# Two row buffers in place of three for a group of attention queries, with the rest written over the scaled queries

## The chip, the cores and the metric

The kernel runs on one core of one Trainium2 chip. The metric is the device time of one execution in microseconds. The time before is 1096.12 us, the median of three runs (1095.92 to 1096.5). A profile of one more execution gives the time of every instruction on the five engines: PE (matmuls), DVE, ACT, POOL (each works through its own queue in order) and SP, which only issues DMAs.

## The reference

Two layers with gates work on x (4 batches, 512 tokens, 512 channels) and a context of the same shape. The names below are those of the reference, cut to the steps.

```python
x = x + tanh(g_xattn[0]) * wkv(w, u, k=layernorm(x), v=ctx)          # a scan over the tokens
x = x + tanh(g_ffn[0])   * bitlinear_ffn(layernorm(x), w1, w2, w3)   # 1 bit weights, int8 groups
x = x + tanh(g_xattn[1]) * attention(layernorm(x), ctx, wq, wkv, wp) # 16 heads of 32
x = x + tanh(g_ffn[1])   * ternary(layernorm(x), gamma, W)           # rms norm, ternary weights
# in attention:
q = qdq(x) @ qdq(wq).T + bq            # 512 queries of a batch, 512 channels
attn = softmax(q k^T / sqrt(32))       # per head
out = qdq(attn v) @ qdq(wp).T + bp
```

## The kernel before, in words

The four batches go through four stages each: the scan (`wkv_layer`), the feed-forward layer (`ffn_layer`), the attention (`attention_layer`) and the closing ternary layer (`ternary_layer`). Each stage is a generator, and a planner (`line`, `place`, `run`) takes steps of all of them in the order of places that are written out by hand. So the attention of batch b runs beside the feed-forward layer of batch b+1 and the scan of batch b+2. The Tile framework then puts the recorded instructions into the queues of the engines, by its own estimate of when each could start, with a buffer that is free at that point; `in_turn` and `next_turn` hold matmuls to the recorded order of the steps. A queue runs in order, so an instruction that waits holds back everything behind it on its engine.

Attention of one batch takes the channels in four groups of 128 (four heads each). `project(g)` makes the queries of a group: four bf16 matmuls into `q_ps` (line 162 through the helper `matmul`), then on DVE the scaled queries `at_q` (line 898), on ACT the half `at_half[0]`, which is `at_q` plus the bias rounded to the short float format (line 903), and on DVE the rest, `at_q` plus bias minus that half (line 904). Both halves go to DRAM (`qD`, line 908, two DMAs on SP), from where `fetch_queries` (line 913, through `stack`) brings them back as `at_qR` in the layout of the score matmuls. Groups 0 and 1 are projected ahead of the loop over the 16 units of a batch, group 2 in unit 0 and group 3 in unit 4.

All of these row tiles come from one ring: `row(...)` in `attention_layer` is a tile of 128x512 floats of the pool `att` with the tag `at_row` and `ROWS = 3` buffers. The same ring serves `at_xn` (the normalised input of the attention, lines 219, 222, 231), `at_y` (line 1036, batches 0 and 1) and, in batches 0 and 1, `tf_xn` of the ternary layer. A buffer comes free when its last reader is done: for `at_q` that is line 904, for the halves the DMA that stores them, for `tf_xn` the PE transposes (`qr_ps`, line 165).

The ternary layer of a batch works on four token tiles t. For batches 0 and 1 a tile passes POOL twice (line 219: centred; line 1147: times gamma), DVE for its largest magnitude (line 222) and four small steps on a 128x1 column (lines 1151, 1152, 1159, 1158), ACT for the rounding (line 231), PE for four transposes (`qr_ps`), ACT again (line 238) and PE for `f_ps`; line 1172 adds the result to x and line 1173 stores it. This layer of batch 0 runs while the attention of batch 1 is in its units around group 3, and the layer of batch 1 beside the attention of batch 2.

Other lines that the prediction names: scan: 599 and 634 (DVE scans), 608, 630, 635, 636, 641, 642 (POOL), 640 (DVE reciprocals), 645 (DVE product); feed-forward: 685 (POOL), 745 (ACT), 746 and 750 (DVE), 697 (DVE); attention: 948 (DVE, negated row maximum of the scores), 950 (ACT, exponentials), 970 (ACT, copies the transposed probabilities), 1000 (DVE, output into `at_o`); layer norm: 180 and 207 (POOL), 191, 194, 200 and 204 (DVE).

Of the kernel before, what the change touches and what calls it, by code (L numbers as in the profile page):

```python
# [11 lines left out]
F32R = mybir.dt.float32r  # L12
# [18 lines left out]
def kernel(  # L31
# [99 lines left out]
    def bank(name, dtype=F32):  # L131

        return psum_tile(name, "m", dtype)
# [27 lines left out]
    def matmul(*args, **kwargs):  # L161
        return in_turn(nc.tensor.matmul(*args, **kwargs))  # L162
# [677 lines left out]
    def attention_layer(b, xb, pool, tiles=range(NT)):  # L840
# [5 lines left out]
        lo, n = tiles[0] * P, len(tiles) * P  # L846
# [9 lines left out]
        def row(name, dtype=F32):  # L856
            return pool.tile([P, D], dtype, name=name, tag="at_row", bufs=ROWS)
# [29 lines left out]
        def project(g):  # L887
            qp = bank("q_ps")[:, 0:n]
            for c in range(NC):
                matmul(  # L890
                    qp,
                    lhsT=wqT[:, c, g * P : (g + 1) * P],
                    rhs=xqT[:, c, lo : lo + n],
                    start=(c == 0),
                    stop=(c == NC - 1),
                )
            q = row("at_q")[:, 0:n]
            nc.vector.scalar_tensor_tensor(
                q, qp, sq[:, g : g + 1], sxb[:, lo : lo + n], ALU.mult, ALU.mult
            )  # L900
            half = [row("at_half", F32R)[:, 0:n] for _ in range(2)]
            bias = bqc[:, g : g + 1]
            nc.scalar.activation(half[0], q, AF.Identity, bias=bias)
            nc.vector.scalar_tensor_tensor(
                half[1], q, bias, half[0].bitcast(F32), ALU.add, ALU.subtract
            )
            for i in range(2):
                nc.sync.dma_start(out=qD[b][g][i, :, lo : lo + n], in_=half[i].bitcast(F32))
# [83 lines left out]
        def collect(k):  # L992
# [14 lines left out]
            )  # L1007

        project(0)
        fetch_keys(0)  # L1010
        fetch_values(0)
        fetch_queries(0)
        yield
        project(1)
        fetch_queries(1)
        yield
# [45 lines left out]
        for k in range(len(units) + 2):  # L1062
# [29 lines left out]
            if now:  # L1092
                p, h = units[k]
                if h == 0:
                    if p + 1 < NP:
                        fetch_keys(p + 1)
                    if p % 2 == 0 and p // 2 + 2 < NC:
                        next_turn()
                        project(p // 2 + 2)
                elif p % 2 and p // 2 + 1 < NC:  # L1100
                    fetch_values(p // 2 + 1)
                if k + 2 < len(units):
                    fetch_queries(k + 2)
# [320 lines left out]
```

## Time and profile before

| what | value |
|---|---|
| time, median of 3 runs | 1096.12 us (1095.92 to 1096.5) |
| the profiled execution's own time | 1094.21 us |
| its span, first to last instruction | 1092.4 us |
| PE busy | 943.3 us, 86% of the span |
| DVE busy | 827.0 us, 76% |
| ACT busy | 729.9 us, 67% |
| POOL busy | 320.7 us, 29% |
| mean granted TensorE clock | 0.956 |
| line 904 | 16 instructions, 742/752/1764 ns (min/median/max) |
| line 903 | 16 instructions, 713/724/760 ns |
| line 908, DMA `qD<-at_half` | 32 issues, 2.0/2.2/4.1 us to landing |
| line 219 on `tf_xn` | 8 instructions, 762/768/772 ns |

Busy time of PE is the time in which a matmul is under way; matmuls overlap, so that is not PE at its peak. The granted clock is the share of TensorE's full clock. A line of a timeline gives the start from the beginning of the span, the time of the merged run of instructions, engine, line, operation, output<-inputs, shape and count, and in brackets the idle time of the engine before it with what ended it.

### The profile page before, as it was taken

Reading aid. Unit: us, or ns where it says so; the run is one execution under the profiler, and the core shown is the slowest. Engines: PE = TensorE matmul, PEld = TensorE weight load, DVE = VectorE, ACT = ScalarE, POOL = GpSimd, SP = SyncE. Lnnn points to the kernel's source line nnn. Section 1 sums busy time; section 2 is a strip of 40 time slices with the busy share of each in tenths; the row PEclk is TensorE's granted clock in tenths of the full one; section 3 lists DMA queues with packets and bytes.
Section 4 is the critical chain, followed back from the end, with each engine's and each line's share of the span. In section 5 each row is a group of like instructions: output and inputs, shape, how many; then the busy total and the mean of one; then the engine's idle time right before and its main releaser. Section 6 shows DMA issues by size and latency. Waiting matters only on the chain.

```text
span 1092.4 us, 17928 instructions
## 1 busy us (share of the span) xinstructions
PE 943.3 (86%) x6350; PEld 680.0 (62%) x6380; DVE 827.0 (76%) x1600; ACT 729.9 (67%) x1490; POOL 320.7 (29%) x328
## 2 busy tenths in 40 slices
PE   3879997998879888799997886999999999878975
PEld 2345564565557666677775665677776777655652
DVE  5985548757876899896769898966687866579976
ACT  5656755567545776667877576677685777877863
POOL 3831104423333254621215545412122410100000
PEclk8889999999999999999999798999999999989998
DMA  8188845464445674645576354655574563244311
GB/s 288 39 272 317 323 169 190 144 221 155 154 146 181 221 234 127 231 129 169 185 234 204 121 177 133 204 195 180 184 231 156 184 210 116 59 148 116 116 42 39
DMA packets 85674, 189.68 MB, mean 174 GB/s; under 512 B 12241, under 2 KB 36817, under 8 KB 74577
## 3 DMA queue, kind: packets, MB, share of 16 engines
q1 hardware_dynamic: 85584, 188.53, 51.7%
q8 instruction: 51, 0.84, 0.3%
q14 instruction: 39, 0.31, 0.1%
HBM read 148.65 MB, written 39.85 MB: 173 GB/s over the span
## 4 chain that ended last, share of the span: by engine, by line
PE 49%; DVE 22%; ACT 14%; POOL 5%; issue 5%; DMA 4%; SPq 1%; ACTq 0%; POOLq 0%; DVEq 0%
PE ff_hp L162 15%; PE pt_ps L165 7%; PE ff_acc L162 6%; PE o_ps L162 4%; PE v_ps L162 4%; PE s_ps L162 3%; ACT at_P L950 3%; DVE wk_q L640 3%; ACT at_PT L970 3%; DVE at_nm L948 2%; PE k_ps L162 2%; DVE wk_p L634 1%; PE qr_ps L165 1%; PE tp_ps L165 1%; ACT wk_e L612 1%
## 5 line engine op out<-in xcount | busy, mean ns | idle before, releaser
L162 PE MATMUL ff_hp<-wT,xp 128*128 128x512 f32 x1024 | 275.7, 412 | 6.6 <-DVE ff_z L746 3.7
L162 PEld LDWEIGHTS ff_hp<-wT,xp 128*128 128x128 f32 x1024 | 195.4, 196 | 54.6 <-DVE ff_z L746 5.7
L950 ACT ACTIVATE at_P<-s_ps,at_nm 128x512 f32<-128x512 f32 x256 | 175.0, 690 | 45.2 <-DVE at_nm L948 43.4
L948 DVE TENSOR_REDUCE at_nm<-s_ps 128x1 f32<-128x512 f32 x256 | 166.6, 677 | 38.4 <-PE s_ps L162 37.9
L970 ACT COPY at_PT<-pt_ps 128x512 f32<-128x512 f32 x224 | 131.2, 590 | 72.6 <-PE pt_ps L165 71.9
L685 POOL TENSOR_TENSOR ff_z<-qg_b,qg_s 128x512 f32<-128x512 bf16 x64 | 71.9, 1124 | 314.6 <-ACT qg_b L684 304.7
L165 PE MATMUL pt_ps<-ident,at_P 128*128 128x128 f32 x1024 | 155.4, 280 | 9.0 <-ACT at_PT L970 4.3
L165 PEld LDWEIGHTS pt_ps<-ident,at_P 128*128 128x128 f32 x1024 | 118.1, 142 | 47.3 <-ACT at_PT L970 10.9
L162 PE MATMUL ff_acc<-wT,hr 128*128 128x512 f32 x512 | 137.6, 409 | 5.2 <-DVE hr L697 2.6
L162 PE MATMUL s_ps<-at_kR,at_qR 128*128 128x512 f32 x256 | 103.0, 464 | 24.0 <-ACT at_P L950 17.6
L162 PEld LDWEIGHTS ff_acc<-wT,hr 128*128 128x128 f32 x512 | 92.9, 191 | 26.2 <-DVE hr L697 4.2
L162 PE MATMUL o_ps<-at_PT,at_V 128*32 128x128 f32 x2048 | 75.4, 281 | 4.7 <-ACT at_PT L970 2.8
L162 PEld LDWEIGHTS o_ps<-at_PT,at_V 128*32 128x32 f32 x2048 | 54.8, 111 | 28.6 <-issue 11.6
L746 DVE SCALAR_TENSOR_TENSOR ff_z<-ff_z,ff_hp 128x512 f32<-128x512 f32 x64 | 43.4, 679 | 37.0 <-ACT ff_z L745 36.9
L745 ACT ACTIVATE ff_z<-ff_hp,coef 128x512 f32<-128x512 f32 x64 | 44.1, 688 | 40.5 <-PE ff_hp L162 38.1
L750 DVE SCALAR_TENSOR_TENSOR ff_z<-ff_hp,coef,ff_z 128x512 f32<-128x512 f32 x64 | 47.7, 745 | 30.2 <-PE ff_hp L162 30.1
L684 ACT CAST qg_b<-qg_i 128x512 bf16<-128x512 int8 x80 | 49.3, 617 | 27.4 <-DVE qg_i L680 17.3
L162 PEld LDWEIGHTS s_ps<-at_kR,at_qR 128*128 128x128 f32 x256 | 43.3, 194 | 36.4 <-ACT at_P L950 25.2
L162 PE MATMUL v_ps<-wkvT,cT 128*128 128x512 f32 x128 | 60.5, 618 | 5.5 <-DVE wT L303 2.3
L162 PE MATMUL k_ps<-cT,wkvT 128*128 128x512 f32 x128 | 61.3, 631 | 2.3 <-ACT wk_k L584 1.0
L640 DVE RECIPROCAL wk_q<-wk_q 128x256 f32<-128x256 f32 x32 | 54.5, 1722 | 3.0 <-POOL wk_q L635 1.6
L696 ACT CAST hr<-tp_ps 128x512 fp32r<-128x512 f32 x64 | 37.6, 588 | 21.7 <-PE tp_ps L165 21.7
(180 smaller groups left out, 1669.4 us busy)
## 6 DMA issues: line engine op xcount, KB each, us to landing
wT<-wD SPq DMA_DIRECT2D x72, 1024.0 KB, 5.4
wn<-in_L_ffn_w_dram SPq DMA_DIRECT2D x18, 1024.0 KB, 6.2
at_kR<-kD SPq DMA_DIRECT2D x128, 128.0 KB, 4.0
at_qR<-qD SPq DMA_DIRECT2D x256, 64.0 KB, 2.5
wD<-wT SPq DMA_DIRECT2D x12, 1024.0 KB, 4.2
kD<-k_half SPq DMA_DIRECT2D x16, 512.0 KB, 2.8
qD<-at_half SPq DMA_DIRECT2D x32, 256.0 KB, 2.2
cn<-in_ctx_dram SPq DMA_DIRECT2D x8, 512.0 KB, 5.9
```

Source lines behind the costliest of these rows:

```text
L162: return in_turn(nc.tensor.matmul(*args, **kwargs))
L165: return in_turn(nc.tensor.transpose(*args))
L640: nc.vector.reciprocal(half, half)
L684: nc.scalar.copy(qb, qi)
L685: nc.gpsimd.tensor_tensor(grouped(src), grouped(qb), s.unsqueeze(2).to_broadcast([P, NG, GS]), ALU.mult)
L696: nc.scalar.copy(part[:, 0, :], pt)
L745: nc.scalar.activation(z, hp, AF.Tanh, scale=coef[:, 0:1])
L746: nc.vector.scalar_tensor_tensor(z, z, 1.0, hp, ALU.add, ALU.mult)
L750: nc.vector.scalar_tensor_tensor(z, hp, coef[:, 1:2], z, ALU.mult, ALU.mult)
L948: nc.vector.tensor_reduce(nm, sp, AX.X, ALU.max, negate=True)
L950: nc.scalar.activation(lanes[k, i, t], sp, AF.Exp, bias=nm, accum_out=sums[k][:, t, i : i + 1],)
L970: made[k] = nc.scalar.copy(dst, blocks(pt))
```

## The change

The second of the two halves no longer takes a buffer of its own from the ring. It is the buffer of the scaled queries `q`, seen in the short float format; line 904 reads `q` and writes over it, and the second DMA of line 908 stores it from there. A group takes two buffers of the ring in place of three.

```diff
@@ -898,7 +898,7 @@
             nc.vector.scalar_tensor_tensor(
                 q, qp, sq[:, g : g + 1], sxb[:, lo : lo + n], ALU.mult, ALU.mult
             )
-            half = [row("at_half", F32R)[:, 0:n] for _ in range(2)]
+            half = [row("at_half", F32R)[:, 0:n], q.bitcast(F32R)]
             bias = bqc[:, g : g + 1]
             nc.scalar.activation(half[0], q, AF.Identity, bias=bias)
             nc.vector.scalar_tensor_tensor(
```

## The prediction

> **What bounds the kernel now.** I read the page first, then all waits of PE, then the timelines of PE, DVE, POOL and SP around the groups whose line 904 moves. Shares of engines:
>
> ```profile
> PE 943.3 (86%) x6350; PEld 680.0 (62%) x6380; DVE 827.0 (76%) x1600; ACT 729.9 (67%) x1490; POOL 320.7 (29%) x328
> ```
>
> PE sets the end, and what counts is the places where it waits. The waits of PE (engine, tile, line, releaser: us in total, times, longest us) hold one at which the ring of the change stands:
>
> ```profile
> PE qr_ps L165 <- ACT tf_xn L231: 16.2, 4, 8.6
> ```
>
> The timeline of PE (start, us, operation, in brackets the idle time before it and its releaser) shows this wait of 8.60 us at 661.05, and three spots that the change also reaches:
>
> ```profile
> 661.05 1.11 PE L165 MATMUL qr_ps<-ident,tf_xn 128*128 128x128 f32 x4 [8.60 <-ACT tf_xn L231]
> ...
> 858.91 0.66 PE L165 MATMUL qr_ps<-ident,tf_xn 128*128 128x128 f32 x4
> ...
> 870.53 0.66 PE L165 MATMUL qr_ps<-ident,tf_xn 128*128 128x128 f32 x4 [0.86 <-ACT at_PT L970]
> ...
> 961.64 1.19 PE L162 MATMUL s_ps<-at_kR,at_qR 128*128 128x512 f32 x2 [3.37 <-DMA at_qR<-qD]
> ```
>
> The ring was full at the first: line 904 of group 3 (batch 1) stood at 662.27, behind `qr_ps` of tile 0, because its buffer was that tile's; SP's store of it held SP's queue for 9.6 us from 653.44, and POOL's passes for tiles 1 and 2 came after that, at 663.13.
>
> **What the change moves.** I compared the order in which both built programs issue on each engine. The counts are the same and nothing differs before some 640 us; three places differ: A, tiles of batch 0 beside group 3 of batch 1; B, tiles of batch 1 beside group 3 of batch 2; C, groups 0 and 1 of batch 3.
>
> *Place A.* Line 904 now comes directly behind line 680 of 644.37, and SP's store of the rest goes out one fetch behind the half's (643.67), so the 9.6 us of SP's waiting are gone. PE gains nothing from that: over the whole span it waits for `at_qR` 4.2 us in 3 times, 3.37 of them at 961.64. The buffers are free early, so both POOL passes of tiles 1 and 2 move up, between POOL's line 685 of 646.14 and line 642 of the scan. POOL and DVE before (two timelines):
>
> ```profile
> 646.14 1.49 POOL L685 TENSOR_TENSOR ff_z<-qg_b,qg_s 128x512 f32<-128x512 bf16 x1
> ...
> 652.47 1.26 POOL L642 TENSOR_TENSOR wk_e<-wk_e 128x512 f32<-128x512 f32 x1
> ...
> 658.38 1.62 POOL L608 TENSOR_TENSOR wk_p<-wk_k,wk_o 128x512 f32<-128x512 f32 x1 [2.65 <-DVE wk_o L599]
> ...
> 663.13 1.52 POOL L219 TENSOR_SCALAR tf_xn<-xb,ln_r 128x512 f32<-128x512 f32 x2
> 664.61 2.52 POOL L1147 TENSOR_TENSOR tf_xn<-tf_xn,gamma_b 128x512 f32<-128x512 f32 x2
> ```
> ```profile
> 654.89 0.68 DVE L645 TENSOR_TENSOR wk_e<-wk_e,wk_q 128x512 f32<-128x512 f32 x1
> ...
> 657.09 1.21 DVE L599 TENSOR_TENSOR_SCAN wk_o<-wc,wk_k 128x512 f32<-128x512 f32 x1
> ...
> 658.88 1.15 DVE L1159 TENSOR_TENSOR tf_s<-tf_s,coef 128x1 f32<-128x1 f32 x1
> ...
> 660.03 0.12 DVE L1158 TENSOR_SCALAR tf_s<-tf_s 128x1 f32<-128x1 f32 x1
> ```
>
> POOL ran without a gap from 644.59 to 653.73, so two passes by 0.76 and two by 1.26, 4.04 us, come on top: line 642 ends at 657.77 instead of 653.73. Line 645, which needs it, had 1.16 us in hand (654.89) and moves by 2.88. Behind it on DVE stands the chain that frees line 231 of tile 0 on ACT and so `qr_ps`; it ends with line 1158. On this stretch DVE gets one more line 222 (0.60 from start to start, as at 655.49 to 656.09), and loses line 599, which moves behind line 1158 (1.13, from 657.09 to the next at 658.22), and a line 998 (0.09). Line 1159 took 1.15 us where its fellows take 0.14, and ended with POOL's line 608 (660.00); this pass follows line 599, so it is gone from there: −1.0. Together 2.88 + 0.60 − 1.13 − 0.09 − 1.0 = +1.26. In this stretch PE ran at half clock (the windows: us, busy time of PE, PEld, DVE, ACT, POOL, then the granted clock, the DMA share and GB/s; the last two rows are from the neighbourhood of 834 us):
>
> ```profile
> 656.27:659.68 3.41, 0.00 (x0) 0.00 (x0) 3.41 (x9) 0.62 (x1) 1.30 (x1) 0.50 0.31 75
> ...
> 833.77:837.18 3.41, 1.82 (x12) 1.27 (x11) 3.41 (x10) 2.41 (x6) 0.00 (x0) 1.00 0.00 0
> 837.18:840.59 3.41, 3.41 (x9) 2.31 (x8) 2.72 (x9) 1.36 (x3) 0.00 (x0) 0.50 0.00 0
> ```
>
> The clock stood at 0.50 until 666.51, so 1.26 us of lost PE time are 0.63 us of work at full clock: **+0.63**. Lower bound −1.06: POOL and ACT have tiles 1 to 3 ready earlier, and the two line 231 that stand on ACT near 678 (0.85 and 0.84) leave the queue in front of an `f_ps` that waited 2.2 us there. Upper bound +2.3: one more window at half clock, 3.41/2 = 1.7. I take the middle, since the windows near 675 were busy 1.90 and 2.00 of 3.41 and kept full clock.
>
> The Trainium skill ("SBUF — State Buffer", section "Who interferes with whom") lets the second of a DVE instruction with two inputs in SBUF and a POOL instruction that reads SBUF wait until the first is done. Line 1159's 1.15 us agree, line 219 on `tf_xn`, never over 0.772 us, shows no such wait; by the rule the four passes put among the scan's DVE products would cost still more.
>
> *Place B.* Before, POOL stood idle at the time:
>
> ```profile
> 851.59 1.04 POOL L685 TENSOR_TENSOR ff_z<-qg_b,qg_s 128x512 f32<-128x512 bf16 x1 [7.76 <-ACT qg_b L684]
> ...
> 860.46 1.52 POOL L219 TENSOR_SCALAR tf_xn<-xb,ln_r 128x512 f32<-128x512 f32 x2 [6.76 <-DVE qg_s L676]
> ```
> ```profile
> 855.75 1.29 DVE L948 TENSOR_REDUCE at_nm<-s_ps 128x1 f32<-128x512 f32 x2 [1.57 <-PE s_ps L162]
> ...
> 857.84 0.75 DVE L750 SCALAR_TENSOR_TENSOR ff_z<-ff_hp,coef,ff_z 128x512 f32<-128x512 f32 x1 [0.79 <-PE ff_hp L162]
> 858.50 0.28 DVE L1000 TENSOR_TENSOR at_o<-ot_ps,at_rt 128x128 f32<-128x128 f32 x1
> ```
>
> So POOL's passes cost POOL nothing, but DVE's magnitudes of tiles 1 and 2 (line 222) now stand ahead of the pair of line 948 and wait for POOL: line 685 ends 852.63, then tile 1 (0.77 + 1.29) to 854.69, lines 180 and 207 (0.7 + 0.2) to 855.6, tile 2 (0.77 + 1.29) to 857.7. Line 222 of tile 2 then occupies DVE to 858.4, and the pair of line 948 starts there, 2.65 later than 855.75. Behind it: the pair 1.2, four small steps 0.46, line 750 0.66, line 1000 0.28, each from start to start: line 1000 ends at 861.0 instead of 858.78. `qr_ps` now waits for that line, whose PSUM bank it takes (before, for ACT): PE idles **+2.2**. The window from 857.66 to 861.07 falls from 3.28 us busy to some 1.1. The rows above show a window of 1.82 busy followed by one at 0.50, so I count half a window more, +1.7. Back comes the 0.86 idle at 870.53, as that tile is rounded earlier. Sum 2.2 + 1.7 − 0.86 = **+3.0**; bounds −0.9 (the wait is covered by work that PE takes meanwhile, the payback stays) and +3.9 (no payback); without the clock +1.3.
>
> The Trainium skill ("TensorE: Matmul & The Clock Gate", section "HAM oscillation — how this bites in real kernels") asks for no idle gap above about 3.4 us; by it a gap of 2.2 costs no clock, B is 1.3 and the forecast 1098.7. The row of 833.77, whose longest gap was 0.95 us, speaks against the rule.
>
> *Place C.* DVE now takes line 898 of group 1 ahead of line 904 of group 0 (954.86 and 955.72 before, 0.75 each). Line 898 needs the last `q_ps` matmul (954.80), so line 904 starts near 955.52 instead of 954.86: **+0.66**, which passes the store (2.2 to landing) to the fetch of 958.04 and so to the 3.37 us wait of PE at 961.64. Bounds 0 (ACT's line 903 hides part) and 0.75.
>
> *The write in place* costs nothing by itself: same instruction, same shape, and DVE has others that write over an input in the time of those that don't (line 645, 0.68). No one else reads the scaled queries after line 904; its wait for line 903 stood there already, so no new wait is added.
>
> *Sum.* 0.63 + 3.0 + 0.66 = +4.3 on the profiled execution: 1094.21 + 4.3 = 1098.5 (span 1092.4 + 4.3 = 1096.7). That execution is 1.91 below the median of the runs, and I carry this: **1100.4**. The bounds add to −2.0 (−1.06 − 0.9 + 0) and +6.95 (2.3 + 3.9 + 0.75), so 1094.1 to 1103.1.
>
> **Rivals.** *Slower still* (0.18): A loses a window of clock too, +1.7, in all +6.0: 1102.1. For it: 656.27 is already at 0.50 and more idle follows it; against: the windows near 675 kept full clock.
>
> *Nothing to be measured* (0.22): the ring still has three buffers, so the change only renames who waits, or B's 2.2 us straddle two windows, cost no clock, and A's round-off earlier pays: 1.3 + 0.66 − 1.06 = +0.9, some 1097. For it: DVE at B has 1.57 and 0.79 idle ahead of the lines concerned; against: 4.04 us of POOL work in a stretch with no gap.
>
> *Faster* (0.14), the other side: POOL's moved passes hide. If line 642 still ends before 654.89, DVE's chain at A is shorter by 1.13 + 0.09 + 1.0 − 0.60 = 1.62, PE restarts at 659.4, ahead of the window border 659.68, and gets full clock one window earlier (1.7); the 1.62 count half (0.81), B gives only its payback, −0.86, C takes 0.66: −2.7, 1093.4. It decides from 1.16 us of added POOL time on. For it: POOL idles 2.83 us ahead of 644.59 and 1.9 after 653.73; against: the order puts tile 1 behind line 685 of 646.14, where no gap is.
>
> **How the numbers follow.** Forecast 0.46, slower still 0.18, nothing 0.22, faster 0.14. A measurement tells 0.2%, 2.2 us, from no change. The sum's bounds, 1094.1 to 1103.1, leave out the faster case and small ends. Faster by over 0.2% is that case, 0.14; within 0.2% the second rival and a little of the forecast's lower end, 0.24; slower 0.62.
>
> **What would show it.** Profile after: line 642 near 656.5 and `qr_ps` near 662.3 with over 9 us of idle (A); the pair of line 948 near 858.4, `qr_ps` near 861 behind an idle time of 2 us and a window at 0.50 behind it (B); `s_ps` near 962 plus what A and B added (C); SP's 9.6 us gone. It is wrong if the scheduler's early tiles free PE from waits after 663 that I bounded at 2 us, or if the clock of a window goes otherwise than the rows above let expect.

## The result and the profile after

| | before | after |
|---|---|---|
| median of the runs | 1095.72 us (16 runs, 1093.12 to 1096.5) | 1097.79 us (16 runs, 1095.98 to 1100.57) |
| profiled execution, span | 1094.21 us, 1092.4 us | 1097.88 us, 1096.0 us |

The ratio is 1.0025, 95% interval 1.0016 to 1.0033: slower by about 2.7 us. A second comparison in other runs gave 1.0025 again (1.0016 to 1.0034); one of its runs took 1629.73 us at a mean clock of 0.72, is a slow one, and is left out here and below. The forecast was 1100.4 us, range 1094.1 to 1103.1.

The shares of the engines hardly move; the instructions are the same:

```profile
PE 942.4 (86%) x6350; PEld 679.7 (62%) x6380; DVE 827.7 (76%) x1600; ACT 731.3 (67%) x1490; POOL 320.9 (29%) x328
```

The waits of PE after the change (engine, tile, line, releaser: us in total, times, longest us) show the known wait grown from 8.6 to 9.9 us, and one that was not there before:

```profile
PE qr_ps L165 <- ACT tf_xn L231: 17.9, 4, 9.9
...
PE qr_ps L165 <- DVE at_o L1000: 2.3, 1, 2.3
```

The timeline of PE gives their places, A and B, and the matmuls after the third place, C (start, us, operation, idle time before it and its releaser):

```profile
662.89 1.11 PE L165 MATMUL qr_ps<-ident,tf_xn 128*128 128x128 f32 x4 [9.88 <-ACT tf_xn L231]
...
860.52 0.66 PE L165 MATMUL qr_ps<-ident,tf_xn 128*128 128x128 f32 x4 [2.33 <-DVE at_o L1000]
...
964.72 1.19 PE L162 MATMUL s_ps<-at_kR,at_qR 128*128 128x512 f32 x2 [4.16 <-DMA at_qR<-qD]
```

How late is PE? I matched the runs of matmuls of the two profiles in their order and took the difference of their starts. From 282 to 645 us it stays within 0.25 us. Then: +0.99 between 645 and 700 us (A), −1.59 between 830 and 850, +2.87 between 850 and 875 (B), +0.97 between 951 and 975 (C), and 0.34 from 1069 us on; together the 3.6 us of the spans. The −1.59 is a window of the clock: the profile of before has TensorE's clock at half speed from 837.18 to 840.59, and this one has not; other profiles have it either way (below).

### The profile page after: what moved, and what is told of

Read it like the earlier page. It is cut to its first block, busy times and chain, and to the rows that moved or that the text cites. A ratio compares the mean times of both kernels' runs of the same rounds, so it can differ in the third digit from the quotient of the medians.

```text
span 1096.0 us, 17923 instructions
## 1 busy us (share of the span) xinstructions
PE 942.4 (86%) x6350; PEld 679.7 (62%) x6380; DVE 827.7 (76%) x1600; ACT 731.3 (67%) x1490; POOL 320.9 (29%) x328
## 4 chain that ended last, share of the span: by engine, by line
PE 46%; DVE 24%; ACT 13%; POOL 6%; DMA 5%; issue 5%; SPq 1%; POOLq 0%; ACTq 0%; DVEq 0%
PE ff_hp L162 14%; PE pt_ps L165 7%; PE ff_acc L162 5%; PE o_ps L162 4%; PE s_ps L162 4%; DVE wk_q L640 3%; ACT at_P L950 3%; PE v_ps L162 3%; ACT at_PT L970 2%; DVE at_nm L948 2%; PE k_ps L162 2%; DVE wk_p L634 2%; PE qr_ps L165 1%; PE tp_ps L165 1%; DVE qg_i L680 1%
## 5 line engine op out<-in xcount | busy, mean ns | idle before, releaser
L750 DVE SCALAR_TENSOR_TENSOR ff_z<-ff_hp,coef,ff_z 128x512 f32<-128x512 f32 x64 | 47.7, 746 | 30.1 <-PE ff_hp L162 29.9
L950 ACT ACTIVATION_READ_ACCUMULATOR at_P<-s_ps,at_nm 128x1 f32 x256 | 52.2, 204 | 0.0
```

The source lines that it names most:

```text
L750: nc.vector.scalar_tensor_tensor(z, hp, coef[:, 1:2], z, ALU.mult, ALU.mult)
L950: nc.scalar.activation(lanes[k, i, t], sp, AF.Exp, bias=nm, accum_out=sums[k][:, t, i : i + 1],)
```

## The experiments

Each run's span times its mean granted clock is called the time at full clock below, the rest of the span the clock's part. This is an account and no cause: a half window in which PE waits anyway counts in the clock's part and costs little. "The whole change" is the changed kernel.

**One batch at a time.** The in-place write is given to one batch only; the other batches keep three buffers.

```diff
-            half = [row("at_half", F32R)[:, 0:n], q.bitcast(F32R)]
+            half = [row("at_half", F32R)[:, 0:n], q.bitcast(F32R) if b == 0 else row("at_half", F32R)[:, 0:n]]
```

(and `b == 1`, `b == 2`, `b == 3`). Batch 0 alone changes no engine's order, batch 1 alone changes it at A only, batch 2 at B only, batch 3 at C only.

> The rest is written in place in batch 0 alone (4 of the 16 groups); in this kernel no engine's order of instructions differs from the kernel before. Theory (the write itself is free, only moved work costs): time as before, ratio 1.000 within 0.001, no place of PE later than before by over 0.3 us beyond what the clock's windows do, line 904 at 742 to 752 ns as before. Rival 1 (writing over an input costs: line 904 slower, or the DMA of the scaled queries' buffer waits longer): a quarter of the 2.7 us, ratio near 1.0006, and line 904 of batch 0 longer.

> In place in batch 1 alone: only the order around group 3 of batch 1 moves (place A). Theory: qr_ps near 662.9 behind 9.9 us of idle in place of 661.05 and 8.6; half of the 1.84 is lost (half clock), then DVE's and POOL's scan stays about 1.0 us late to 690 us and takes PE with it: PE +1.0 us from 690 on, ratio near 1.0009; whether the window at half clock near 837 us comes is open (1.6 us less if not). Rival 2 (the places add nothing by themselves, the 2.7 us come of the clock's windows alone): no steady lag of PE behind 690 us. Rival 1: 0.7 us spread over four line 904.

> In place in batch 2 alone: only the order around group 3 of batch 2 moves (place B). Theory: PE idles 2.2 to 2.4 us ahead of qr_ps near 860, released by DVE line 1000; a window at half clock behind it (1.6 us) if the window that holds the idle time has PE busy under 2 us; 0.9 back at the next qr_ps. PE +2.9 us from 873 on with the clock, +1.3 without, ratio near 1.0026 or 1.0012. Rival 1: +0.7, no idle there. Rival 2: no idle there, a lag that changes only at windows of the clock.

> In place in batch 3 alone: DVE takes line 898 of group 1 ahead of line 904 of group 0, nothing else moves (place C). Theory: s_ps near 961.6 comes 0.66 to 0.85 us later, by the later line 904 through the store and the fetch, and the lag stays to the end: ratio near 1.0007. Rival 1: the same 0.7 us, but from longer line 904, not from their order. Rival 2: no lag at 961.

Measured, with lateness of PE against the profile of before by stretch of the span, and in brackets what of it a different number of windows at half clock makes at most (half of their length; where PE has waits to fill it is less, as A of batches 2 and 3 shows, where no order moves):

| in place in | ratio, 95% interval | 645 to 700 (A) | 850 to 875 (B) | idle ahead of `s_ps` near 961 (C) |
|---|---|---|---|---|
| batch 0 | 1.0007 (0.9997 to 1.0016) | +0.02 (0) | −0.03 (0) | 4.21 |
| batch 1 | 1.0001 (0.9990 to 1.0013) | +2.95 (1.71) | −0.03 (0) | 4.41 |
| batch 2 | 1.0022 (1.0011 to 1.0033) | +1.24 (1.71) | +2.84 (1.70) | 4.57 |
| batch 3 | 1.0004 (0.9990 to 1.0018) | +1.20 (1.71) | −0.03 (0) | 4.19 |
| all | 1.0025 (1.0016 to 1.0033) | +0.99 (0) | +2.87 (1.71) | 4.16 |

The write itself is free as far as these runs tell: with batch 0 alone no order moves, and the median of line 904 stays at 0.75 us (0.752 before, 0.751 for its four in place here, 0.750 after with all 16 in place). Its ratio of 1.0007 alone could not tell this from the rival's 1.0006. But PE is late neither at A nor at B, and these runs have 1044.8 ± 0.5 us at full clock beside 1045.2 ± 0.3 of the kernel before on the same chip. At C PE is 0.5 us late, against the expectation, though nothing moves there in this kernel; more on that below. The new wait belongs to batch 2 alone, as the timelines of PE show, batch 1 first, then batch 2:

```profile
660.38 1.11 PE L165 MATMUL qr_ps<-ident,tf_xn 128*128 128x128 f32 x4 [9.87 <-ACT tf_xn L231]
...
857.66 0.66 PE L165 MATMUL qr_ps<-ident,tf_xn 128*128 128x128 f32 x4
```
```profile
659.95 1.11 PE L165 MATMUL qr_ps<-ident,tf_xn 128*128 128x128 f32 x4 [8.60 <-ACT tf_xn L231]
...
861.10 0.66 PE L165 MATMUL qr_ps<-ident,tf_xn 128*128 128x128 f32 x4 [2.31 <-DVE at_o L1000]
```

The rival that the clock's windows alone make the 2.7 us falls: B's idle time has an engine and a line. But the windows make the runs of any one kernel spread, by up to 1.7 us for each window, and so no ratio of these four tells less than about 1 us.

C was expected at +0.66 to 0.85 and fails. With the order changed PE's idle time there is 4.16, 4.47, 4.19, 4.10, 4.34 and 4.01 us in six profiles, mean 4.21; with the order of before it is 3.37, 4.21, 4.41, 3.52, 4.57 and 4.23, mean 4.05. The means differ by 0.16, with a standard error of 0.21. The profile of before, 3.37, was the shortest of all twelve. SP's timelines, of before and then of the whole change, say why the later line 904 does not count:

```profile
954.86 1.12 SPq L908 DMA_DIRECT2D qD<-at_half  x2
...
958.04 1.98 SPq L913 DMA_DIRECT2D at_qR<-qD  x4
```
```profile
957.15 0.34 SPq L908 DMA_DIRECT2D qD<-at_half  x1
958.56 0.34 SPq L908 DMA_DIRECT2D qD<-at_q  x1
...
961.09 1.98 SPq L913 DMA_DIRECT2D at_qR<-qD  x4
```

SP's first fetch of `at_qR` starts when the first store, that of the half, has landed (957.15 and 3.9 us to landing; 954.86 and 3.2 before). That store leaves right behind line 903, where it left before, 0.06 us after the last `q_ps` matmul in both profiles. Only the store of the rest is later (1.41 us behind the first in place of 0.78), and it has landed at 961.71, before SP comes to the third of the four fetches, 1.2 us after the first in either profile. What does vary is the landing of the first store: 3.2 us in the profile of before, 3.3 in the second one of batch 1, and 3.85 to 4.23 in the other ten. Both short ones have the order of before; whether the new order ever has one, six profiles don't show.

**B: is it the magnitude of tile 2?** The whole change, with that one line 222 kept behind the pair of line 948:

```diff
-        nc.vector.tensor_reduce(dst, src, AX.X, ALU.max, apply_absolute_value=True)
+        return nc.vector.tensor_reduce(dst, src, AX.X, ALU.max, apply_absolute_value=True)
...
-    exps = {}
+    exps = {}; held = lambda ins, name, yes: behind(ins, exps[name]) if yes else None
...
-            nc.vector.tensor_reduce(nm, sp, AX.X, ALU.max, negate=True)
+            exps["nm"] = nc.vector.tensor_reduce(nm, sp, AX.X, ALU.max, negate=True)
...
-            absmax(s[:, 0:1], xn)
+            held(absmax(s[:, 0:1], xn), "nm", b == 1 and t == 2)
```

> The whole change, but at place B the magnitude of tile 2 alone (one line 222 of batch 1) is kept behind the pair of line 948 that it stood in front of; POOL's and SP's orders are those of the whole change. Theory (that one instruction, waiting for POOL's second pair of passes, holds the pair and so line 1000 and qr_ps): PE's idle time of 2.3 us ahead of qr_ps near 860 falls below 0.4, no window at half clock near 861 to 864, PE near 873 about 2.4 to 2.9 us earlier than in the whole change; ratio to before 1.000 to 1.001. Rival (POOL's early passes slow DVE's two-input operations there, or tile 1 in front is enough): idle time of 1.5 us or more stays, ratio 1.002 or more.

The ratio is 0.9993 (0.9984 to 1.0001): the whole loss is gone, though POOL still makes its passes early and A and C are as in the whole change. The timeline of PE and the windows (us, busy PE, PEld, DVE, ACT, POOL, then the granted clock, DMA share, GB/s):

```profile
857.74 0.66 PE L165 MATMUL qr_ps<-ident,tf_xn 128*128 128x128 f32 x4 [0.52 <-ACT at_PT L970]
```
```profile
855.04:858.46 3.42, 2.90 (x22) 2.40 (x21) 2.52 (x7) 3.16 (x9) 1.22 (x1) 1.00 0.97 410
858.46:861.87 3.41, 3.41 (x45) 2.71 (x44) 2.74 (x6) 3.09 (x8) 2.07 (x2) 1.00 0.42 173
```

No half window follows, and PE is 0.53 us earlier over 850 to 875 than before. The idle time of 0.52 was expected below 0.4, a small miss with another releaser. A and C still stand in this kernel, and it is at most 0.1 us slower than before; with the 0.53 us that PE gains at B set against it, the two cost 0.6 us together at most.

**A: POOL's passes or line 904?** The whole change, with tile 2's passes kept behind line 642 (`held` is as above, and `centred_aside` returns its instruction):

```diff
-            nc.gpsimd.tensor_tensor(A, A, E, ALU.add)
+            exps["sum"] = nc.gpsimd.tensor_tensor(A, A, E, ALU.add)
...
-            centred_aside(xn, xb, r, t)
+            held(centred_aside(xn, xb, r, t), "sum", b == 0 and t in (1, 2))
```

(For tile 1 the line 642 that is held to lies an earlier chunk back, so only tile 2 moves.)

> The whole change, but at place A POOL's first pass of tile 2 of batch 0 (line 219, and with it line 1147) is kept behind line 642 of the scan; tile 1's two passes stay ahead. Theory (POOL's added passes set line 642, it sets line 645, and that the chain of line 1158): line 642 ends about 2.0 us earlier (near 655.9 in place of 657.90), qr_ps comes near 661.0 to 661.4 in place of 662.89. Rival (line 904, put ahead on DVE at 645 and lengthened to 1.77 us beside POOL, sets the delay): qr_ps stays near 662.5 to 662.9. The time: at most 0.9 us less than the whole change, too little for the rounds.

The ratio is 1.0033 (1.0015 to 1.0051), no better than the whole change, as was expected of so small an edit. Line 642 ends at 656.18 (expected 655.9) and line 645 starts at 656.27 in place of 657.93, 1.66 us earlier. But `qr_ps` comes at 662.20, with 9.07 us of idle in place of 9.88, neither the theory's 661.0 to 661.4 nor the rival's 662.5 to 662.9. The timelines of DVE and POOL of this kernel show where the other 1.0 us went:

```profile
657.68 1.17 DVE L676 TENSOR_SCALAR qg_s<-qg_s 128x8 f32<-128x8 f32 x1
...
660.84 0.14 DVE L1158 TENSOR_SCALAR tf_s<-tf_s 128x1 f32<-128x1 f32 x1
```
```profile
656.16 1.28 POOL L219 TENSOR_SCALAR tf_xn<-xb,ln_r 128x512 f32<-128x512 f32 x1
657.52 1.26 POOL L1147 TENSOR_TENSOR tf_xn<-tf_xn,gamma_b 128x512 f32<-128x512 f32 x1
```

Line 676 takes 0.16 us in the whole change and 1.17 here; it ends with POOL's pass that the edit put beside it (658.85 and 658.78). So line 642 does set line 645, as the theory has it, and the passes of tile 2 cost at both spots that were tried.

**A without its wait.** In the kernel before, tile 0's magnitude ends at 640.48, and its four small steps stand behind the scan until 657.07. Recording the steps of batch 0 one step earlier, with the transposes where they were:

```diff
             yield True
-            yield True
+            if b: yield True
             absmax(s[:, 0:1], xn)
...
         rounded(xn, s[:, 1:2])
         yield True
+        if b == 0: yield True
```

> The kernel before (three buffers), with the magnitude, the four small steps and the rounding of batch 0's ternary tiles recorded one step earlier, the PE transposes where they were. Theory (at place A PE waits 8.6 us only because DVE takes tile 0's four small steps behind the scan, 16 us after its magnitude at 640): qr_ps of tile 0 follows tp_ps near 652.5 without that wait, PE's next wait is for the exponentials near 655; the idle time falls from 8.6 to 3 to 4 us and the clock's windows at half go with it; 4 to 7 us less, ratio 0.994 to 0.996. Rival (PE has to wait there for the scores' exponentials and the scan anyway): qr_ps early, but the idle time comes back at the next matmuls, ratio 0.999 to 1.000.

> Two buffers (the whole change), tile 2 held at place B as in the first run of this call, and batch 0's ternary chain one step earlier as in the third. Theory: both repairs add, and with A's wait gone POOL's early passes no longer stand in front of anything PE waits for: 4 to 7 us less than before, ratio 0.994 to 0.996, at least as good as the three buffers with the early chain. Rival: POOL's early passes still hold line 645 and the scan, 1 to 2 us worse than the third run.

Ratios 0.9970 (0.9961 to 0.9980) and 0.9972 (0.9962 to 0.9982): both beat both kernels of the case, the one before by some 3 us, less than the 4 to 7 expected. Medians are 1091.77 and 1090.72 us, beside 1094.54 of the kernel before on the same chip. The timeline of PE, three buffers with the early chain:

```profile
652.24 0.66 PE L165 MATMUL qr_ps<-ident,tf_xn 128*128 128x128 f32 x4
653.79 0.94 PE L162 MATMUL s_ps<-at_kR,at_qR 128*128 128x512 f32 x2 [0.90 <-ACT at_P L950]
...
686.99 0.66 PE L165 MATMUL qr_ps<-ident,tf_xn 128*128 128x128 f32 x4 [3.93 <-ACT at_PT L970]
```

The wait of 8.6 us is gone, but pieces come back, 3.93 us of them ahead of 686.99, so the rival is half right. What stays is the clock: the clock's part is 43.1 us in these runs (standard error 0.6) and 44.3 with two buffers (0.7), beside 47.2 in the kernel before, and the time at full clock is not shorter (1046.5 ± 0.7 and 1045.1 ± 0.6 beside 1045.4 ± 0.2). With the early chain, two buffers (and B repaired) or three make no difference that these runs tell.

**How A's lateness ends.** Two more runs, all and batch 1 alone:

> The whole change once more, on one chip with batch 1 alone. In each run the span times the mean granted clock is the time at full clock, and the rest of the span is what the clock took. Theory (A costs 1.0 us of time at full clock and gets about as much back in the clock's windows, B costs 1.3 us at full clock and 1.7 us of the clock, C nothing): ratio 1.002 to 1.003, time at full clock 2 to 3 us above the kernel before, the clock's part within 1.5 us of it. Rival (A keeps its 1.0 us and the first comparison drew lucky windows): ratio 1.0035 or more.

> In place in batch 1 alone (place A), once more. Theory: ratio 1.000 within 0.001; time at full clock about 1.0 us above the kernel before, the clock's part about 1 us below it. Rival (A keeps its 1.0 us): ratio 1.001 or more, the clock's part as before.

The ratios are 1.0025 (1.0016 to 1.0034) and 1.0001 (0.9990 to 1.0013). Means over all runs, with standard errors (those of the kernel before are from three chips, 1045.2 to 1045.6 us at full clock):

| kernel, runs | time at full clock | the clock's part |
|---|---|---|
| before, 87 | 1045.4 ± 0.2 us | 47.2 ± 0.2 us |
| batch 1 alone, 23 | 1046.4 ± 0.3 | 46.4 ± 0.3 |
| batch 2 alone, 12 | 1047.8 ± 0.5 | 47.0 ± 0.6 |
| whole change, 26 | 1048.2 ± 0.3 | 47.7 ± 0.3 |
| whole, tile 2 held at B, 11 | 1046.6 ± 0.6 | 45.4 ± 0.4 |

A alone adds 1.0 ± 0.4 us of time at full clock, and the clock's part falls by 0.8 ± 0.4: what is left, 0.2, is within the error. B adds the rest. Two things stay open. In which windows A gets its 0.8 us back isn't shown: of six profiles with A's order one has the half window near 837 us, of the four others with the same program up to there two have it. (In the first pair the windows begin at the same times, and PE's work, 1.0 us later, left it busy 2.14 us of the window ahead in place of 1.82.) And B's half window stands in all four profiles with its idle time (whole change twice, batch 2, tile 2 held at A) and in none of the other eight. Holding tile 2 there takes 2.3 ± 0.5 us of clock's part and 1.6 ± 0.7 at full clock off the whole change, yet batch 2 alone has all of its 2.4 ± 0.5 us at full clock and none in the clock's part. The two parts move against each other from run to run (correlation −0.76 in the kernel before), so how B's cost divides between wait and clock is shown by the profiles only.

## Why the prediction was right, step by step

*Place B, +3.0: right in mechanism, and in size by the profiles.* The order put line 222 of tiles 1 and 2 in front of the pair; the timelines of DVE and the windows of the whole change:

```profile
854.22 0.69 DVE L222 TENSOR_REDUCE tf_s<-tf_xn 128x1 f32<-128x512 f32 x1 [1.34 <-POOL tf_xn L1147]
...
857.27 0.69 DVE L222 TENSOR_REDUCE tf_s<-tf_xn 128x1 f32<-128x512 f32 x1 [1.79 <-POOL tf_xn L1147]
857.88 1.28 DVE L948 TENSOR_REDUCE at_nm<-s_ps 128x1 f32<-128x512 f32 x2
...
860.18 0.28 DVE L1000 TENSOR_TENSOR at_o<-ot_ps,at_rt 128x128 f32<-128x128 f32 x1
```
```profile
857.66:861.07 3.41, 1.08 (x10) 0.85 (x8) 3.38 (x11) 2.48 (x6) 0.00 (x0) 1.00 0.96 404
861.07:864.49 3.42, 3.42 (x12) 2.77 (x12) 3.25 (x6) 2.93 (x7) 2.05 (x2) 0.50 0.03 5
```

This profile runs 0.6 us ahead of that of before here. PE loses 2.20 at `qr_ps` (2.2 forecast), 1.61 in the half window (1.7), and gets 0.94 back by the next `qr_ps` (0.86): 2.87. In the times of the runs batch 2 alone costs 2.4 us (1.2 to 3.6). The choice between the rows and the Trainium skill's rule ("TensorE: Matmul & The Clock Gate", section "HAM oscillation — how this bites in real kernels") fell to the rows: the gap of 2.33 us, well under the rule's 3.4, was followed by half clock.

*Place A, +0.63: the idle time was mis-sized, and what stays of it is less.* PE came 1.84 us later, not 1.26. Line 642 ended at 657.90 (forecast 657.77) and the chain's last, line 1158, at 661.67, 1.52 us later than before; the missing part is line 684, which now waits on ACT for DVE's later line 680 (the row names line 1152, which follows line 680 on DVE at once) and stands in front of line 231. The timelines of POOL, DVE and ACT of the whole change:

```profile
656.65 1.25 POOL L642 TENSOR_TENSOR wk_e<-wk_e 128x512 f32<-128x512 f32 x1
```
```profile
657.93 0.69 DVE L645 TENSOR_TENSOR wk_e<-wk_e,wk_q 128x512 f32<-128x512 f32 x1 [1.71 <-POOL wk_e L642]
...
660.72 0.68 DVE L680 TENSOR_TENSOR qg_i<-ff_z,qg_r 128x512 int8<-128x512 f32 x1
...
661.52 0.15 DVE L1158 TENSOR_SCALAR tf_s<-tf_s 128x1 f32<-128x1 f32 x1
```
```profile
661.50 0.62 ACT L684 CAST qg_b<-qg_i 128x512 bf16<-128x512 int8 x1 [5.04 <-DVE tf_s L1152]
662.02 0.81 ACT L231 ACTIVATE tf_xn<-tf_xn,magic,tf_s 128x512 f32<-128x512 f32 x1
```

That half clock halves it was right: the clock came back at the same 666.5 us in both profiles, and PE was 0.99 late at 666.83. Early tiles then paid nearly all of it back by 682 (0.14), as the lower bound allowed; but the scan, 1.0 us late on DVE, took PE with it at 690.61 (+1.00). The prediction followed `qr_ps` and not the scan behind it. Over many runs the clock's part falls by about that much.

The prediction also said that line 219 shows no wait beside DVE. In this stretch it does, in the timelines of DVE and POOL of the whole change:

```profile
644.96 1.78 DVE L904 SCALAR_TENSOR_TENSOR at_q<-at_q,bqc,at_half 128x512 fp32r<-128x512 f32 x1
...
647.26 0.93 DVE L632 TENSOR_TENSOR wk_q<-wk_e,wk_q 128x512 f32<-128x512 f32 x1
...
649.30 1.87 DVE L634 TENSOR_TENSOR_SCAN wk_p<-wk_e 128x512 f32<-128x512 f32 x1
```
```profile
644.60 1.59 POOL L630 TENSOR_TENSOR wk_e<-wk_e,wk_v 128x512 f32<-128x512 f32 x1 [2.85 <-issue]
...
647.62 1.21 POOL L219 TENSOR_SCALAR tf_xn<-xb,ln_r 128x512 f32<-128x512 f32 x1
...
650.04 2.20 POOL L1147 TENSOR_TENSOR tf_xn<-tf_xn,gamma_b 128x512 f32<-128x512 f32 x1
```

Line 904 takes 1.78 in place of 0.75 and ends 0.55 after POOL's line 630 does; line 219 takes 1.21 in place of 0.77 beside line 632; the pass of 2.20 in place of 1.26 ends 1.07 after line 634's 651.17. That is what the Trainium skill says ("SBUF — State Buffer", section "Who interferes with whom"): the one that comes second waits. Line 642 came only 0.13 us later than forecast all the same: line 635, which took 2.19 us before, took 1.29 here.

*Place C, +0.66: this step failed.* "Line 904 starts near 955.52 instead of 954.86 ... which passes the store (2.2 to landing) to the fetch": line 904 did start 0.6 us later, but the fetch of 958.04 waited for the other store, that of line 903's half, which the change leaves where it was; the rest's, sent at 955.64, landed at 958.65, after the fetch had begun. Mean idle times of 4.21 and 4.05 us differ by 0.16 ± 0.21. That the first pair shows PE +0.97 late here, near the forecast, is luck of the landings.

*The write in place, 0: right*, by batch 0 alone. *SP's freed queue, 0: right*: its wait for line 904 fell from 9.6 to 2.2 us, and SP then waits for PE (the next load of weights) up to 11.3 us.

*The sum.* 4.3 forecast, 2.7 measured; 0.6 + 3.0 + 0.7 against about 0, 2.9 (2.4 in the times of batch 2 alone) and 0.2 ± 0.2. The likeliest case held, and the side and the place that matter were right; that two of the three terms were too large did not show in the range, as B is most of the sum. Of the 2.6 us between 1100.4 and 1097.79, 0.4 are the base (1096.12 in three runs, 1095.72 in sixteen) and 2.2 the sum, as the medians differ by 2.07.

## What to carry to other kernels

A buffer given back early is also an order given to the scheduler: work that had waited for the buffer moves ahead on queues that run in order, and a short instruction waiting there for a slow engine holds those behind it. So look at what stands behind the first reader of the freed buffer, here one reduction of 0.7 us that waited 1.8. And where runs of one kernel differ by windows of the clock worth up to 1.7 us each, compare places in several profiles, not two spans: a difference read off one pair (place C, and the window at 837) may belong to the pair.

## What the runs showed of the hardware

TensorE's granted clock is decided window by window, 3.41 us each, on a grid whose start differs among executions (the first half window behind 645 us begins between 653.41 and 658.14 in the ten profiles without the early chain; before and after happen to share one grid). In twelve profiles, from 300 to 1085 us, 2546 windows began at full clock and were followed by a whole one at full or half. All 105 in which PE was busy less than 1.6 us were followed by half clock; none of the 2367 with more than 1.9 us was; of the 74 between, 38 stayed and 36 fell. So it is the share of the window, near one half, that decides, and not the longest gap in it: windows whose longest gap was 0.8 to 0.9 us fell, and one with 1.8 us stayed. A wait of 2 us costs a window or not by where the grid cuts it: the 2.2 us ahead of `f_ps` near 677 were followed by half clock in the profiles of batch 2, batch 3 and tile 2 held at A, and in those of before and of the whole change they were not. That this makes the whole spread among runs of a kernel isn't shown; what the early chain gains stands in the clock's part.
